# Start-up of a conditioned ternary feed-forward kernel: conditions loaded first, the second block's gathers moved, some work moved to ScalarE, a shorter alpha

## The chip, the core and the metric

The kernel runs on one core of one Trainium2 chip. The core has five engines that run side by side[...]: PE (TensorE, matrix products), DVE (VectorE), ACT (ScalarE), POOL (GpSimd) and SP (SyncE, which here only issues DMAs). [...] The metric is the time of one execution on the device in microseconds; the median over three runs was 1069.36 us, the lowest 1067.48 and the highest 1070.88.

## What is computed

A batch `x` of 128 x 64 x 512 floats is multiplied, sample by sample, with a 64 x 64 matrix that a condition index picks out of a table of 200. The result goes through a feed-forward network of width 512 - 2048 - 512 whose two weight matrices are first made ternary: each weight becomes -alpha, 0 or +alpha. The output of the network is rounded to 15 levels and added to `x`.

```python
def ternarize(W, threshold):
    absW = jnp.abs(W)
    delta = threshold * jnp.max(absW)
    mask = absW > delta
    n = jnp.maximum(jnp.sum(mask), 1)
    alpha = jnp.sum(jnp.where(mask, absW, 0.0)) / n
    Wt = alpha * jnp.sign(W) * mask
    return W + jax.lax.stop_gradient(Wt - W)

h = einsum('bct,bcd->bdt', x, weights[conditions])
h = gelu(ternary_linear(h, W1, b1), exact)
y = ternary_linear(h, W2, b2)
scale = max(abs(y)) / 7 + 1e-8
out = x + clip(round(y / scale), -7, 7) * scale
```

Alpha needs a maximum over the whole matrix (for delta), then a count and a sum over what lies above it. Since sum(|W| over the mask) = sum(relu(|W| - delta)) + n * delta, alpha can be written as sum(relu) / n + delta.

## The kernel before

**Blocks.** The 128 samples are 16 blocks (`NB`) of 8 samples; a block is 4 pairs (`PAIRS`) and 512 columns (`BLK`). For a block, `mix` multiplies each pair's `x` by a block-diagonal matrix `diag` that holds two condition matrices; `hi` and `lo` split the product into two parts of reduced precision (ACT copies, DVE subtracts). Layer 1 has 16 steps (`hc`, `NH` = 16) of 8 matmuls, one per 128 hidden units; ACT's `bend` applies the gelu with `alpha[1]` as scale and copies the result to its high part, and a subtraction on DVE or POOL (`low`) makes the low part. Layer 2 has 16 steps of 8 matmuls that add up in four banks of PSUM.

**Weights.** Both matrices are kept in small types and have to be widened to fp32r just before use: `widen1(n, hc)` for a step of layer 1 into one of four buffers `w1f`, `widen2(n, hc)` for one of layer 2 into one of four buffers `w2f`. All these widenings are POOL's before the change. A buffer comes free when the matmul four steps earlier has read it.

**Block 0 is a ramp.** No step can start until W1's threshold is known, so block 0 has an order of its own, written out by hand; every engine's instructions keep the order in which the program makes them (`InOrder`). SP loads W1 (four groups of 1 MB, `nat1`), the first `x`, then W2. PE runs 54 products on constants (`idle`) while DVE reduces W1 to its maximum and ACT makes signs and magnitudes. `fetch` is a gather of one pair's condition matrices, an indirect DMA that POOL issues from indices `rows`, which DVE works out of `conditions`; `place` copies a gathered pair into `diag` in two halves. Then, for W1: `mask1` (|W| > delta), `signed1` (mask times sign, the ternary matrix), `count1` (PE sums the mask), `above1` (ACT sums relu(|W| - delta)) and `alpha_1`. The products of layer 1 (`early`) do not need alpha, only the gelu after them does; five PSUM slots hold products that wait, so `early(k)` needs the gelu of step k - 5.

**After alpha** a loop over `hc` 5 to 15 (lines 639 to 645) issues `early(hc)`, the widening of step hc + 2, the bend of step hc - 4, and in `behind(hc)` the preparation of W2 on DVE: its maximum (`largest2`), delta, and `signed2(g)`, the ternary form of group g in two instructions over 128 x 2048. Even steps' `low` is POOL's in this ramp, odd steps' is DVE's. Layer 2 of block 0 follows as a loop of 14 steps (lines 658 to 683), in which DVE still makes groups 2 and 3 of W2, ACT keeps both matrices in fp8 (`kept`) and counts W2 (`count2`), and the next block's four pairs are mixed (`condition(1, j)`) at steps 5, 7, 9 and 11. Block 1 then starts with its layer 1.

**What the change touches.** The load of `conditions` (line 127, issued by ACT), the four calls `fetch(1, j)` (lines 558, 569, 576) with their `place` (line 624, steps 6 to 9 of the ramp's loop), W1's fourth sum, which DVE makes with a product of magnitude and mask (lines 593 to 602) while ACT makes the other three, `widen1` (line 383), `alpha_1` (lines 488 to 501), `sign1(3)` (line 580), `early(3)` (line 605), the two first `widen2` (lines 634 to 637).

Of the kernel before, what the change touches and what calls it, by code (L numbers as in the profile page):

```python
# [29 lines left out]
F32 = mybir.dt.float32  # L30
# [6 lines left out]
ALU = mybir.AluOpType  # L37
AX = mybir.AxisListType
PSUM = bass.MemoryType.PSUM

P = 128
# [17 lines left out]
def tile_cond_ternary_ffn(  # L59
# [12 lines left out]
    pe, act, dve, pool, sp = (  # L72
        InOrder(tc, e) for e in (nc.tensor, nc.scalar, nc.vector, nc.gpsimd, nc.sync)
    )
    B, C, T = x.shape
# [4 lines left out]
    PAIRS = 4  # L80
    BLK = PAIRS * P
    NB = B // (2 * PAIRS)
    NG = 4
# [6 lines left out]
    const = ctx.enter_context(tc.tile_pool(name="const", bufs=1))  # L90
# [3 lines left out]
    ps_c = ctx.enter_context(tc.tile_pool(name="ps_c", bufs=2, space=PSUM))  # L94
# [29 lines left out]
    first = big.tile([P, 4, P], F32, tag="big", name="first")  # L124
    cond_i, cond_f, wrap = (first[:, i, : B // 2] for i in range(3))
    cond_i = cond_i.bitcast(I32)
    act.dma_start(out=cond_i, in_=conditions)


    nat1, nat2 = [], []  # L130
# [4 lines left out]
    for g in range(NG):  # L135
        w = big.tile([P, GH, T], F32, tag="big", name=f"nat1_{g}")
# [6 lines left out]
    for g in range(NG):  # L143
        w = big.tile([P, GH, T], F32, tag="big", name=f"nat2_{g}")
# [40 lines left out]
    def fetch(n, j):  # L185

        pair = n * PAIRS + j
        wg = gather.tile([P, D], F32, tag="wg", name=f"wg_{pair}")
        pool.indirect_dma_start(
            out=wg[:, :],  # L190
            out_offset=None,
            in_=table,
            in_offset=bass.IndirectOffsetOnAxis(ap=rows[:, pair : pair + 1], axis=0),
        )
        return wg

    def place(j, wg):
        for h in range(2):
            pool.tensor_copy(diag[half_of(h), j, h * D : (h + 1) * D], wg[half_of(h), :])
# [49 lines left out]
    def alpha_of(w, sums, count):  # L249

        dve.tensor_scalar(count, count, 1.0, None, ALU.max)
        dve.reciprocal(count, count)
        alpha = const.tile([P, 1], F32, name=f"alpha_{w}")
        dve.tensor_tensor(alpha, sums, count, ALU.mult)
        return alpha

    def flat(w):
        return w.rearrange("p a b -> p (a b)")
# [3 lines left out]
    masks = [big.tile([P, 2, WCH], BF16, tag="big", name=f"masks_{i}") for i in range(2)]  # L262
    terns = [big.tile([P, 2, WCH], BF16, tag="big", name=f"terns_{i}") for i in range(2)]
    junk = big.tile([P, 2, WCH], BF16, tag="big", name="junk")
    above, above_last = junk[:, 0, :], junk[:, 1, :]
    top_1 = const.tile([P, sum(map(len, PIECES))], F32)
    sums1 = const.tile([P, NG], F32)

    def group1(tiles, g):
        return tiles[g // 2][:, g % 2, :]  # L270

    def sign1(g):
        act.activation(group1(signs, g), flat(nat1[g]), AF.Sign)
# [9 lines left out]
    mags = []  # L283
# [54 lines left out]
    def signed1(g, part=slice(0, WCH)):  # L338
        dve.tensor_tensor(
            group1(terns, g)[:, part],  # L340
            group1(masks, g)[:, part],
            group1(signs, g)[:, part],
            ALU.mult,
        )

    def count1(g, number, first, final):
        n = number.shape[1]
        for i in range(WCH // n):
            pe.matmul(
                out=number,  # L350
                lhsT=ones_b,
                rhs=group1(masks, g)[:, i * n : (i + 1) * n],
                start=(first and i == 0),
                stop=(final and i == WCH // n - 1),
            )
# [22 lines left out]
    def widen1(n, hc):  # L378

        if n == 0:  # L380
            w = w1f[hc % 4]
            g, i = divmod(hc, GH)
            pool.tensor_copy(flat(w), group1(terns, g)[:, i * T : (i + 1) * T])
        else:
            w = w1f[hc % 2]
            pool.tensor_copy(flat(w), w1t[:, hc])
        wide1[n, hc] = w

    def widen2(n, hc):
        if n == 0 and hc < NH - LAG:  # L390
            w = w2f[hc % 4]
        elif n == NB - 1 and hc == NH - 1:

            w = flat(w1f[0])
        else:
            w = w2f[hc % 2]
        if n == 0 and hc < NH - LAG:
            g, i = divmod(hc, GH)
            pool.tensor_copy(w, group1(terns2, g)[:, i * T : (i + 1) * T])
        else:  # L400
            pool.tensor_copy(w, w2t[:, hc])
        wide2[n, hc] = w
# [33 lines left out]
    def layer2(n, hc, js=range(PAIRS)):  # L436
        two = hidden[n, hc]
        w = wide2[n, hc]
        if n not in ypsum:
            ypsum[n] = [  # L440
                ps_y.tile([P, T], F32, tag=f"py{j}", name=f"py{j}_{n}") for j in range(PAIRS)
            ]
        for j in js:
            for k in range(2):
                pe.matmul(
                    out=ypsum[n][j],
                    lhsT=two[k][:, j * P : (j + 1) * P],
                    rhs=w,
                    start=(hc == 0 and k == 0),
                    stop=(hc == NH - 1 and k == 1),  # L450
                )
# [19 lines left out]
    def early(hc, between=None):  # L471

        slot = (hc + 1) % 5
        if slot < 2:
            ph = ps_h.tile([P, BLK], F32, tag="ph", name=f"ph_0_{hc}")
        else:
            ph = ps_y.tile([P, BLK], F32, tag=f"py{slot - 2}", name=f"ph_0_{hc}")
        layer1(0, hc, ph, 2 if hc == 0 else 1, between)
        waiting[hc] = ph
# [8 lines left out]
    def alpha_1():  # L488

        count = const.tile([P, 1], F32, name="count1")  # L490
        dve.tensor_reduce(count, number, AX.X, ALU.add)
        yield
        total = ps_c.tile([P, NG], F32, tag="pc", name="total1")
        pe.matmul(out=total, lhsT=ones_f, rhs=sums1, start=True, stop=True)
        count_last = const.tile([P, 1], F32, name="count1_last")
        dve.tensor_reduce(count_last, number_last, AX.X, ALU.add)
        kept = const.tile([P, 1], F32, name="kept1")
        dve.tensor_reduce(kept, total, AX.X, ALU.add)
        dve.scalar_tensor_tensor(kept, count, delta1, kept, ALU.mult, ALU.add)
        dve.tensor_tensor(count, count, count_last, ALU.add)  # L500
        alpha[1] = alpha_of("w1", kept, count)

    top_2 = const.tile([P, NG], F32)
    delta = []
# [50 lines left out]
        alpha[2] = alpha_of("w2", both[:, 0:1], both[:, 1:2])  # L555


    fetched = [fetch(1, 0)]
    mask1(0, parts1[0])
    signed1(0, parts1[0])  # L560
    widen1(0, 0)
# [4 lines left out]
    hi0(3)  # L566
    lo0(2)
    lo0(3)
    fetched += [fetch(1, 1)]
    early(0)  # L570
    early(1)
    mask1(0, parts1[1])
    signed1(0, parts1[1])
    widen1(0, 2)
    widen1(0, 3)
    fetched += [fetch(1, j) for j in range(2, PAIRS)]
    abs1(3)
    for g in range(NG - 1):
        above1(g)
    sign1(3)  # L580
    number = ps_y.tile([P, T // 2], F32, tag="py3", name="number")
    count1(0, number, True, False)
    mask1(1)
# [3 lines left out]
    mask1(3)  # L587
    early(2)
    count1(1, number, False, False)
    count1(2, number, False, True)  # L590
    number_last = ps_c.tile([P, T // 2], F32, tag="pc", name="number_last")
    count1(3, number_last, True, True)
    dve.tensor_tensor_reduce(
        out=above_last,
        in0=flat(mags[3]),
        in1=group1(masks, 3),
        scale=1.0,
        scalar=0.0,
        op0=ALU.mult,
        op1=ALU.add,  # L600
        accum_out=sums1[:, 3:4],
    )
    find = alpha_1()
    next(find)
    early(3, lambda: next(find, None))
    signed1(2)
    widen1(0, 5)
    early(4)
    early_bend(0)
# [10 lines left out]
    def behind(hc):  # L620
        if 5 <= hc < 5 + NG:
            largest2(hc - 5)
        if 6 <= hc < 6 + PAIRS:
            place(hc - 6, fetched[hc - 6])
        if hc == 9:
            signed1(3)
        if hc == 11:
            delta.extend(next(find))
            signed2(0)
        if hc == 12:  # L630
            low(0, 1)
            low(0, 3)
            signed2(1)
        if hc == 14:
            widen2(0, 0)
        if hc == 15:
            widen2(0, 1)

    for hc in range(5, NH):
        ahead(hc)  # L640
# [17 lines left out]
    for hc in range(NH - LAG):  # L658
        if hc + 2 < NH - LAG:
            widen2(0, hc + 2)  # L660
        layer2(0, hc)
        if hc == 0:
            signed2(2)
        if hc == 1:
            for i in (13, 14, 15):
                low(0, i)
        if hc < NG:
            kept(w1t, hc, terns)
        if hc == 3:
            signed2(3)  # L670
        if hc == 4:
            two_next = parts(1)
            w2t = big.tile([P, NH, T], F8, tag="big", name="w2t")
        if 4 <= hc < 4 + 2 * NG:
            g = (hc - 4) // 2
            if hc % 2 == 0:
                count2(g)
            else:
                kept(w2t, g, terns2)
        if hc in (5, 7, 9, 11):  # L680
            j = (hc - 5) // 2
            condition(1, j, pair_of(x_next, j), two_next)
            sum2(j)
    cond[1] = two_next
# [401 lines left out]
```

## Time and profile before

| What | Value |
|---|---|
| median of three runs | 1069.36 us |
| the profiled execution's own time | 1069.97 us |
| its span | 1067.9 us |
| PE busy | 991.2 us, 93% of the span |
| DVE busy | 613.4 us, 57% |
| ACT busy | 610.0 us, 57% |
| POOL busy | 635.3 us, 59% |
| first matmul of layer 1 in block 0 | 22.57 us after the span's start |
| alpha of W1 written | 35.86 us |
| first matmul of layer 2 in block 0 | 61.58 us |
| first matmul of block 1 | 92.33 us |

A row of a timeline gives the start in us from the span's start, the duration, the engine, line of the program, operation, tiles and shapes, how many instructions are merged into the row, and in brackets how long the engine had been idle and what ended that. Nearly all instructions pass through one helper on line 55, so the tile names tell them apart, not the line. `wf` stands for the widened weights of both layers, `py` for the sums of layer 2, `ph` for those of layer 1, `terns` for the ternary matrices, `wg` for a gathered pair of condition matrices, `h` for the split gelu outputs. [...]

### The profile page before, as it was taken

What the parts mean: (1) busy time and instruction counts of PE and PEld (TensorE: products, weight loads), DVE (VectorE), ACT (ScalarE), POOL (GpSimd) and SP (SyncE); (2) the same over time, 40 slices, a digit from 0 to 9 for tenths busy, and PEclk for the clock granted to TensorE, in tenths of its full rate; (3) what the DMA queues carried; (4) which work ended last, traced back from release to release, by engine and by line L of the source; (5) the groups of instructions that cost most, each with busy time, mean ns of one, the idle gap of its engine ahead of it and who ended that gap; (6) DMA issues with size and microseconds to landing.
All of it is one profiled execution on the core that took longest, in us unless ns stands there. A gap on an engine that the chain in (4) does not pass through costs nothing.

```text
span 1067.9 us, 16731 instructions
## 1 busy us (share of the span) xinstructions
PE 991.2 (93%) x5765; PEld 866.0 (81%) x5765; DVE 613.4 (57%) x1080; ACT 610.0 (57%) x1038; POOL 635.3 (59%) x1019
## 2 busy tenths in 40 slices
PE   8989999999999999999999999999999999999400
PEld 4778889999999999999999999999898888888300
DVE  6996736565656656565666655666655223231682
ACT  6875446656666666666666665666555334334481
POOL 4884747576666667576666767576664435333242
PEclk9999999999999999999999999999999999999855
DMA  9100010000000010101000010100001010041899
GB/s 369 46 21 1 14 32 5 30 15 22 23 23 23 14 32 5 31 15 30 16 22 24 14 32 4 34 13 30 16 21 42 3 40 6 1 148 31 301 412 367
DMA packets 26611, 62.20 MB, mean 58 GB/s; under 512 B 3488, under 2 KB 3488, under 8 KB 25760
## 3 DMA queue, kind: packets, MB, share of 16 engines
q1 hardware_dynamic: 19728, 42.22, 11.7%
q0 software_dynamic: 6656, 18.88, 4.6%
q8 instruction: 47, 0.77, 0.3%
q14 instruction: 36, 0.29, 0.1%
q10 hardware_dynamic: 144, 0.03, 0.0%
HBM read 44.34 MB, written 16.78 MB: 57 GB/s over the span
## 4 chain that ended last, share of the span: by engine, by line
PE 88%; DMA 3%; POOL 3%; DVE 2%; ACT 1%; issue 1%; SPq 1%; POOLq 0%; DVEq 0%; ACTq 0%
PE py L55 44%; PE xy L55 16%; PE z L55 12%; PE ph L55 11%; PE pc L55 5%; DMA xt<-in_x 2%; POOL wf L55 2%; DVE y L55 1%; ACT diag L55 1%; POOL wg L55 1%; POOL h L55 1%; SPq L55 1%; DMA wg<-in_L_cond_weights,rows 1%; DMA first<-in_itok_B 0%; POOL diag L55 0%
## 5 line engine op out<-in xcount | busy, mean ns | idle before, releaser
L55 PE MATMUL py<-wf,h 128*128 128x512 f32 x2048 | 532.6, 396 | 3.6 <-POOL wf L55 2.7
L55 PEld LDWEIGHTS py<-wf,h 128*128 128x128 f32 x2048 | 366.4, 189 | 68.8 <-POOL wf L55 3.2
L55 DVE TENSOR_TENSOR h<-ring,h 128x512 fp32r<-128x512 f32 x249 | 193.7, 780 | 184.0 <-ACT h L55 184.0
L55 POOL CAST wf<-w2t 128x512 fp32r<-128x512 fp8e4 x242 | 174.4, 721 | 151.7 <-PE py L55 147.7
L55 ACT ACTIVATE ring<-ring,b1t,alpha_w 128x512 f32<-128x512 f32 x176 | 144.4, 820 | 97.7 <-DVE ring L55 97.7
L55 POOL CAST wf<-w1s 128x256 fp32r<-128x256 fp8e4 (+1 forms) x264 | 133.8, 511 | 109.8 <-PE xy L55 80.6
L55 POOL CAST wf<-w1t 128x256 fp32r<-128x256 fp8e4 (+1 forms) x240 | 157.1, 659 | 56.3 <-PE ph L55 45.3
L55 ACT CAST h<-ring 128x512 fp32r<-128x512 f32 x256 | 158.9, 621 | 8.2
L55 PE MATMUL ph<-x,wf 128*128 128x512 f32 (+1 forms) x648 | 158.5, 389 | 1.1 <-POOL wf L55 1.0
L55 ACT ACTIVATE ring<-ph,b1t,alpha_w 128x512 f32<-128x512 f32 x80 | 62.3, 779 | 145.5 <-PE ph L55 141.9
L55 PEld LDWEIGHTS ph<-x,wf 128*128 128x128 f32 x648 | 119.7, 188 | 27.9 <-POOL wf L55 3.0
L55 DVE TENSOR_TENSOR ring<-xy,ring 128x256 f32<-128x256 f32 (+1 forms) x176 | 97.4, 553 | 64.2 <-PE xy L55 64.2
L55 PEld LDWEIGHTS xy<-xt,wf 128*128 128x128 f32 x704 | 107.6, 189 | 14.1
L55 PE MATMUL xy<-xb,wf 128*128 128x256 f32 x704 | 112.4, 282 | 0.0
L55 PE MATMUL xy<-xt,wf 128*128 128x256 f32 x704 | 111.8, 282 | 0.0
L55 PEld LDWEIGHTS xy<-xb,wf 128*128 128x128 f32 x704 | 102.3, 190 | 7.6
L55 ACT COPY ring<-xy 128x256 f32<-128x256 f32 x176 | 65.0, 369 | 68.1 <-PE xy L55 68.1
L55 PE MATMUL z<-xt,wf 128*128 128x256 f32 x704 | 98.6, 283 | 0.0
L55 ACT COPY ring<-z 128x512 f32<-128x512 f32 x88 | 51.7, 588 | 73.6 <-DVE h L55 73.0
L55 PEld LDWEIGHTS z<-xt,wf 128*128 128x128 f32 x704 | 90.5, 191 | 0.0
L55 DVE TENSOR_TENSOR xt<-x_quarters,xt 128x512 fp32r<-128x512 f32 x44 | 33.8, 768 | 91.0 <-ACT xt L55 91.0
L55 POOL DMA_INDIRECT wg<-in_L_cond_weights,rows x64 | 76.3, 1193 | 14.9 <-DVE rows L55 4.7
(106 smaller groups left out, 860.4 us busy)
## 6 DMA issues: line engine op xcount, KB each, us to landing
xt<-in_x SPq DMA_DIRECT2D x36, 512.0 KB, 9.0
out<-y POOLq DMA_DIRECT2D x30, 512.0 KB, 13.1
x_quarters<-in_x SPq DMA_DIRECT2D x48, 256.0 KB, 2.6
nat<-in_L_ffn_W SPq DMA_DIRECT2D x6, 1024.0 KB, 6.2
nat<-in_L_ffn_W SPq DMA_DIRECT2D x3, 512.0 KB
wg<-in_L_cond_weights,rows POOLq DMA_INDIRECT x64, 2.7
w1t<-in_x SPq DMA_DIRECT2D x4, 256.0 KB, 2.6
w2t<-in_x SPq DMA_DIRECT2D x4, 256.0 KB, 2.6
```

The lines of the kernel that those rows point to most:

```text
L55: return lambda *args, **kw: self._tc.keep_in_program_order(make(*args, **kw))
```

## The change

The load of `conditions` moves from ACT's queue to the head of SP's. The gathers of block 1 leave the ramp; they are issued in steps 0 to 3 of layer 2 of block 0 and placed in steps 4 to 7, and `condition(1, j)` and `sum2(j)` move one step back, to 6, 8, 10 and 12. W1's fourth sum is made by ACT like the other three, and `sign1(3)` moves behind it to step 6 of the ramp's loop. The widenings of steps 7, 9, 11, 13 and 15 of layer 1 in block 0 are ACT's. All four counts add into one bank, and alpha is sum * (1 / count) + delta, with the reciprocal taken before the sum is there. `early(3)` comes ahead of the last two counts, and `signed1(2)` ahead of the last steps of alpha. The first two `widen2` are issued one step earlier in the ramp's loop.

```diff
-    act.dma_start(out=cond_i, in_=conditions)
+    sp.dma_start(out=cond_i, in_=conditions)
...
-            pool.tensor_copy(flat(w), group1(terns, g)[:, i * T : (i + 1) * T])
+            src = group1(terns, g)[:, i * T : (i + 1) * T]
+            if hc > 6 and hc % 2 == 1:
+                act.copy(flat(w), src)
+            else:
+                pool.tensor_copy(flat(w), src)
...
         dve.tensor_reduce(count, number, AX.X, ALU.add)
+        dve.tensor_scalar(count, count, 1.0, None, ALU.max)
+        dve.reciprocal(count, count)
         yield
         total = ps_c.tile([P, NG], F32, tag="pc", name="total1")
         pe.matmul(out=total, lhsT=ones_f, rhs=sums1, start=True, stop=True)
-        count_last = const.tile([P, 1], F32, name="count1_last")
-        dve.tensor_reduce(count_last, number_last, AX.X, ALU.add)
         kept = const.tile([P, 1], F32, name="kept1")
         dve.tensor_reduce(kept, total, AX.X, ALU.add)
-        dve.scalar_tensor_tensor(kept, count, delta1, kept, ALU.mult, ALU.add)
-        dve.tensor_tensor(count, count, count_last, ALU.add)
-        alpha[1] = alpha_of("w1", kept, count)
+        alpha[1] = const.tile([P, 1], F32, name="alpha_w1")
+        dve.tensor_scalar(alpha[1], kept, count, delta1, ALU.mult, ALU.add)
...
-    fetched = [fetch(1, 0)]
...
-    fetched += [fetch(1, 1)]
...
-    fetched += [fetch(1, j) for j in range(2, PAIRS)]
     abs1(3)
-    for g in range(NG - 1):
+    for g in range(NG):
         above1(g)
-    sign1(3)
...
-    count1(2, number, False, True)
-    number_last = ps_c.tile([P, T // 2], F32, tag="pc", name="number_last")
-    count1(3, number_last, True, True)
-    dve.tensor_tensor_reduce(
...
-    )
+    early(3)
+    count1(2, number, False, False)
+    count1(3, number, False, True)
     find = alpha_1()
     next(find)
-    early(3, lambda: next(find, None))
     signed1(2)
+    next(find, None)
...
-        if 6 <= hc < 6 + PAIRS:
-            place(hc - 6, fetched[hc - 6])
+        if hc == 6:
+            sign1(3)
...
-        if hc == 14:
-            widen2(0, 0)
-        if hc == 15:
-            widen2(0, 1)
+        if hc in (13, 14):
+            widen2(0, hc - 13)
...
         layer2(0, hc)
+        if hc < PAIRS:
+            fetched.append(fetch(1, hc))
+        elif hc < 2 * PAIRS:
+            place(hc - PAIRS, fetched[hc])
...
-        if hc in (5, 7, 9, 11):
-            j = (hc - 5) // 2
+        if hc in (6, 8, 10, 12):
+            j = (hc - 6) // 2
```

## The prediction

> **What bounds the kernel now.** I read the page first (PE is 93% busy, and 88% of the chain that ended last), then the chain of waits in order of time, then the timeline of the first 95 us. From 92.33 us on, where block 1 starts, the chain is PE matmuls end to end, and the change touches nothing there. So the end moves by what the start of block 1 moves: everything has to be read from the ramp.
>
> ```profile
> PE 88%; DMA 3%; POOL 3%; DVE 2%; ACT 1%; issue 1%; SPq 1%; POOLq 0%; DVEq 0%; ACTq 0%
> ```
>
> In the ramp PE stands still where POOL's widened weights come late, most of all ahead of layer 2. The timeline there shows why they are late:
>
> ```profile
> 53.41 2.79 DVE L55 TENSOR_TENSOR h<-ring,h 128x512 fp32r<-128x512 f32 x2
> ...
> 53.93 1.73 POOL L55 TENSOR_TENSOR h<-ring,h 128x512 fp32r<-128x512 f32 x1
> ...
> 55.60 1.07 POOL L55 CAST wf<-terns 128x512 fp32r<-128x512 bf16 x1
> 56.12 1.63 DVE L55 TENSOR_SCALAR junk<-nat,minus_w 128x2048 bf16<-128x2048 f32 x1
> ...
> 56.64 2.27 POOL L55 TENSOR_TENSOR h<-ring,h 128x512 fp32r<-128x512 f32 x1
> ...
> 57.79 3.27 DVE L55 SCALAR_TENSOR_TENSOR terns<-nat,delta_w,junk 128x2048 bf16<-128x2048 f32 x1
> 58.85 3.69 POOL L55 CAST wf<-terns 128x512 fp32r<-128x512 bf16 x2
> ...
> 61.58 1.89 PE L55 MATMUL py<-wf,h 128*128 128x512 f32 x5 [2.74 <-POOL wf L55]
> ```
>
> DVE and POOL take turns. The cast ends at 56.67 and the DVE row that began at 56.12 ends 1.08 later (57.75); POOL's low part ends 1.16 after that (58.91), DVE's next 2.15 after that (61.06), the next cast 0.46 later, and PE starts. Each "long" instruction is mostly a wait for the other engine. The **exclusive prices** are thus 1.08 for `signed2`'s first instruction, 2.15 for its second, 0.54 for a low part on DVE (56.20 minus 55.66), 1.16 for one on POOL, 0.46 for a cast. While DVE is full, from 49.6 to 77 us, POOL gets one instruction per DVE instruction.
>
> The gap costs twice. The windows around it show the granted clock in the column behind the five engines:
>
> ```profile
> 58.60:61.60 3.00, 0.26 (x3) 0.03 (x1) 3.00 (x2) 2.69 (x3) 3.00 (x3) 1.00 0.00 0
> 61.60:65.80 4.20, 4.20 (x12) 3.29 (x13) 4.20 (x5) 4.20 (x4) 4.20 (x4) 0.59 0.41 125
> 65.80:68.00 2.20, 2.20 (x11) 1.83 (x10) 2.16 (x2) 1.71 (x1) 2.20 (x3) 1.00 0.00 0
> ```
>
> After 2.74 us without work PE ran 4.2 us at 0.59: 4.2 x 0.41 = **1.7 us lost**.
>
> **The change, part by part.**
>
> *Conditions on SP.* The DMA took 5.3 us to land from ACT's queue, beside W1's; at the head of an idle SP queue it should take no more than the 2.6 of a 256 KB quarter of `x`. SP's whole queue (W1, x, b1, W2, b2) is issued 0.4 later, one issue. The indices come 2.5 to 3 us earlier, so gathers and `place` are done before they are needed. DVE's maximum no longer waits for the indices (it began at 7.21, with W1 there at 5.9): 0.9 earlier. But PE's 54 constant products still end at 16.95, where the transposition of the maximum started before too, so delta stays. What gains is the mixing: it waited for `diag` at 18.16 and 19.53, and can now run 17.2 to 20.9. Layer 1 then begins at 20.9 instead of 22.57; its second half waits for the fourth low part, 22.3 instead of 23.82. **Gain 1.5 us** at that point. If the conditions land no earlier, this goes.
>
> *Alpha.* PE is full from there: step 1, four counts of 0.85 and steps 2 and 3 end at 32.6. ACT's four sums (2.1 each) end at 31.9, hidden behind that. Then DVE's count (0.42), two small ones (0.4), `signed1(2)` (1.2, newly ahead of alpha), two small ones (0.4): alpha at 35.2, against 35.86. The product of magnitude and mask (2.29) and three tiny instructions are gone, but 1.2 is put in their place and PE's step 3 in front: **gain 0.7**.
>
> *ACT in the loop.* Before, gelu and copy took 1.33 per step against PE's 1.82, with room. New are five casts (no such row on ACT; nearest are `h<-ring` at 0.62, stepping by 0.54, and a four times larger `w1t<-terns` at 1.9; I take 0.55) and `sign1(3)` (1.9) inside the loop. `early(8)` waits for gelu 3, behind that sign: 0.9 of PE idle. `early(11)` lands at 48.7, against 48.60: **the gain is spent**. Copy 8 ends at 35.2 + 9 x 1.34 + 1.9 + 4 x 0.55 = 51.4, against 49.36. The five casts leave POOL (five times 0.6 to 2.7), so the ramp's last steps no longer stall for POOL (0.58 and 2.74 before): `early(15)` ends at 57.8, and layer 2 begins at 58.5, when gelu 13 has freed its bank. **Gain 3.1**, and without the long gap also the 1.7 of slow clock.
>
> *Gathers into layer 2.* Here it is given back. Delta of W2 comes with `early(11)`, so DVE's full stretch starts at about 50.2, no earlier than before (49.59). Then, in turns: first `signed2` 1.1 + 2.25, low 8 1.15, 0.54, cast 0.46, 0.54, low 10 1.15, 1.1, cast 0.46, 2.15, low 12 1.15, 0.54, cast 0.46: the third `widen2` is there at 63.3, and step 2 of layer 2, wanted at 62.1, starts then. Now the four gathers stand between the next four casts. Their rows before:
>
> ```profile
> 28.80 2.24 POOL L55 DMA_INDIRECT wg<-in_L_cond_weights,rows  x1
> 31.35 2.72 POOL L55 DMA_INDIRECT wg<-in_L_cond_weights,rows  x1 [0.30 <-issue]
> ...
> 108.40 2.70 DVE L55 TENSOR_TENSOR w1s<-w1t 128x2048 fp8e4<-128x2048 fp8e4 x1
> 109.10 2.83 POOL L55 DMA_INDIRECT wg<-in_L_cond_weights,rows  x1
> 111.94 0.99 POOL L55 CAST wf<-w1t 128x512 fp32r<-128x512 fp8e4 x1
> ```
>
> Undisturbed a gather takes 0.97; at 109.10 it waits until DVE ends (111.10) and needs 0.83 more, in which DVE's next instruction starts, and the cast behind it waits for that one. So each gather costs a turn. From 63.3: gathers end at 64.7, 67.6, 70.8, 73.6, and the casts between them at 65.6, 69.4, 71.7, 75.5. Layer 2's steps 3 to 6 start at those four times instead of every 1.82: PE idles 0.5, 2.0, 0.5, 2.0. Step 6 starts at 75.5. From there eight steps (14.56) and four mixings (3.56) run without a stall (places cost two times 0.3, DVE is idle by then). The last mixing is now followed by one step of layer 2 (1.82) instead of two, which has to cover its high and low part (0.59 and 0.69 plus two hand-overs, some 1.45): it just does, and if ACT or DVE is late by more than 0.35, block 1 waits for the rest. Block 1 at **93.7, against 92.33: 1.4 later**.
>
> [...] The row at 109.10, a two-input DVE instruction, has the gather wait; I follow the row.
>
> **The sum:** 1069.97 for the profiled execution plus 1.4 is 1071.4. That execution lies 0.6 above the median, so on the median's scale I forecast **1070.8**: no change that can be told, since 0.3% (3.2 us) is what a measurement of this kernel tells from none.
>
> **Rivals.**
>
> *Faster: the feed keeps up.* If gathers fit between DVE's instructions, layer 2 runs through from 63.4: 12 x 1.82 + 3.56 gives 88.8, 3.5 earlier: 1065.8. If casts 1 and 2 come early too, from 57.8 straight through it is 86.9: 1064. For it: layer 2 is ready 3.1 earlier and the slow clock is gone. Against it: the row at 109.10, and eight more POOL instructions where it already takes turns.
>
> *Slower: the clock drops again.* Same starvation, but the two gaps of 2.0 count as idle. Each would cost 1.7 if PE were the limit behind it; the first is half hidden by the next wait for a cast, the second, ahead of step 6, is not. 1070.8 + 1.7 is 1072.5, with both nearly 1073.5. It decides if a gap of 2.0 suffices. [...] here 2.74 was enough, [...] and 2.0 is not safe.
>
> *The head gains nothing:* conditions land after 5 us all the same, or W1's later issue shows. Then alpha is about 1 later and all behind it: 1071.8 to 1072.3.
>
> **Numbers.** My forecast's own range is 1069 to 1072.5 (the turns are known to a few tenths each, the ACT cast to 0.1, five times). Chances: forecast 0.43 with the head case in it, feed keeps up (wholly or partly) 0.36, slow clock 0.21. The range for 8 in 10 reaches to both: 1065 to 1073.5. Of the faster case about five sixths passes 3.2 us; of the slower one most stays near the bound. Faster 0.30, same 0.50, slower 0.20.
>
> **What would show it.** Right: conditions landed by 3.5, mixing from about 17, alpha near 35, no PE gap of more than 1 us between 49 and 58, layer 2 from about 58, and gaps for `wf` of 1 to 2 us at its steps 2 to 6, with gathers of 1.4 to 2 us before them. Wrong: gathers of 1.0 there and casts every 1.8 (faster), or a granted clock under 1 between 65 and 80 (slower). Block 1's first matmul, 92.33 before, carries the verdict: whatever it moves, the end moves.

## The result, and the profile after

| What | Before | After |
|---|---|---|
| median of 20 runs each | 1069.30 us (1067.18 to 1070.92) | 1070.05 us (1069.09 to 1071.02) |
| ratio after to before | | 1.0010, 95% interval 1.0004 to 1.0017 |
| profiled execution, own time / span | 1069.97 / 1067.9 us | 1070.15 / 1068.3 us |
| first matmul of layer 1 in block 0 | 22.57 us | 20.70 us |
| alpha of W1 written | 35.86 us | 34.87 us |
| first matmul of layer 2 in block 0 | 61.58 us | 57.50 us |
| first matmul of block 1 | 92.33 us | 93.12 us |

The change costs 0.75 us of 1069. That is 0.1%, just clear of none by the interval of this comparison and far under the 0.3% that the forecast took as its bound; by that bound it is no change, as forecast. Inside the ramp much moved. Layer 2 of block 0 starts 4.1 us earlier, and then takes 35.62 us to reach block 1 instead of 30.75, or instead of some 29.05 if the 1.7 us of half clock are taken out of before. So 5.8 us were won ahead of layer 2 or with the clock, and 6.6 given back inside it. Behind block 1's first matmul all profiles of this document take 974.9 to 976.4 us to the end of the span, so the start of block 1 carries the result to within some 1.5 us.

The chain that ended last, from the page of after. It is still PE, now 91% where it was 88%; POOL's share fell from 3% to 1%.

```profile
PE 91%; DMA 3%; DVE 2%; ACT 2%; POOL 1%; issue 1%; SPq 1%; POOLq 0%; DVEq 0%; ACTq 0%
```

PE's timeline of after: start, duration, operation, how many matmuls (8 are one step), and in brackets the idle time and what ended it.

```profile
20.70 1.32 PE L55 MATMUL ph<-x,wf 128*128 128x256 f32 x9
22.34 2.94 PE L55 MATMUL ph<-x,wf 128*128 128x256 f32 x15 [0.33 <-DVE x L55]
...
35.88 2.08 PE L55 MATMUL ph<-x,wf 128*128 128x512 f32 x8 [1.28 <-ACT ring L55]
...
42.71 5.73 PE L55 MATMUL ph<-x,wf 128*128 128x512 f32 x24 [0.37 <-ACT ring L55]
48.30 9.36 PE L55 MATMUL ph<-x,wf 128*128 128x512 f32 x40
57.50 3.79 PE L55 MATMUL py<-wf,h 128*128 128x512 f32 x16
62.91 4.15 PE L55 MATMUL py<-wf,h 128*128 128x512 f32 x16 [1.62 <-POOL wf L55]
67.44 2.12 PE L55 MATMUL py<-wf,h 128*128 128x512 f32 x8 [0.38 <-POOL wf L55]
71.06 4.13 PE L55 MATMUL py<-wf,h 128*128 128x512 f32 x16 [1.50 <-POOL wf L55]
76.66 1.16 PE L55 MATMUL pc<-diag,xt 128*128 128x128 f32 x8 [1.47 <-POOL diag L55]
...
93.12 1.98 PE L55 MATMUL ph<-x,wf 128*128 128x512 f32 x8
```

Up to 57 us the longest stop is now 1.28 us, behind alpha; the stop of 2.74 us ahead of layer 2 is gone. In its place stand four stops inside layer 2, three for `wf` (a widened weight) and one for `diag` (a placed condition). POOL's timeline in that stretch shows the cause of all but the first:

```profile
63.01 1.25 POOL L55 DMA_INDIRECT wg<-in_L_cond_weights,rows  x1 [0.15 <-issue]
64.28 0.62 POOL L55 CAST wf<-terns 128x512 fp32r<-128x512 bf16 x1
65.06 1.71 POOL L55 DMA_INDIRECT wg<-in_L_cond_weights,rows  x1 [0.17 <-PE py L55]
66.77 0.62 POOL L55 CAST wf<-terns 128x512 fp32r<-128x512 bf16 x1
67.56 2.83 POOL L55 DMA_INDIRECT wg<-in_L_cond_weights,rows  x1 [0.17 <-issue]
70.39 0.62 POOL L55 CAST wf<-terns 128x512 fp32r<-128x512 bf16 x1
71.18 1.23 POOL L55 DMA_INDIRECT wg<-in_L_cond_weights,rows  x1 [0.17 <-issue]
72.41 0.62 POOL L55 CAST wf<-terns 128x512 fp32r<-128x512 bf16 x1
72.98 3.63 POOL L55 COPY diag<-wg 64x64 f32<-64x64 f32 x2
```

And DVE's timeline beside it:

```profile
66.68 2.86 DVE L55 SCALAR_TENSOR_TENSOR terns<-nat,delta_w,junk 128x2048 bf16<-128x2048 f32 x1
69.47 2.70 DVE L55 TENSOR_TENSOR h<-ring,h 128x512 fp32r<-128x512 f32 x3
72.09 2.03 DVE L55 TENSOR_SCALAR junk<-nat,minus_w 128x2048 bf16<-128x2048 f32 x1
74.16 2.35 DVE L55 SCALAR_TENSOR_TENSOR terns<-nat,delta_w,junk 128x2048 bf16<-128x2048 f32 x1
```

Read the third gather with it. It is issued at 67.56 and waits until DVE's row of 66.68 has ended (69.54), then works for 0.85 and ends at 70.39. Only then can the cast for step 5 (counted from 0) run, and PE starts step 5 at 71.06. The last row of POOL is the same wait for a `place`: its second half stands behind the DVE row of 74.16, ends at 76.61, and the mixing starts at 76.66.

### The profile page after: what moved, and what is told of

Its sections match the earlier page's. It is cut to its first block, busy times and chain, and to the rows that moved or that the text cites. A ratio compares the mean times of both kernels' runs of the same rounds, so it can differ in the third digit from the quotient of the medians.

```text
span 1068.3 us, 16722 instructions
## 1 busy us (share of the span) xinstructions
PE 990.0 (93%) x5764; PEld 864.0 (81%) x5765; DVE 610.8 (57%) x1075; ACT 614.4 (58%) x1045; POOL 629.5 (59%) x1014
## 4 chain that ended last, share of the span: by engine, by line
PE 91%; DMA 3%; DVE 2%; ACT 2%; POOL 1%; issue 1%; SPq 1%; POOLq 0%; DVEq 0%; ACTq 0%
PE py L55 43%; PE xy L55 16%; PE ph L55 13%; PE z L55 12%; PE pc L55 5%; DMA xt<-in_x 3%; PE idle L55 1%; DVE y L55 1%; ACT diag L55 1%; SPq L55 1%; POOL wg L55 0%; POOL diag L55 0%; ACT ring L55 0%; PE number L55 0%; DVE ymax L55 0%
```

## The experiments

My theory before the runs: two separate parts of the change gain (conditions, casts on ACT), and the gathers give it back, because each takes one of POOL's turns where POOL feeds PE. The rivals: the start-up parts gain nothing in truth, or what the gathers lose was lost anyway, to DVE's full stretch.

**The change without its move of the gathers.** Gathers, places and mixing stand where they stood before; all else is the change.

```diff
+    fetched = [fetch(1, 0)]
     mask1(0, parts1[0])
...
+    fetched += [fetch(1, 1)]
     early(0)
...
+    fetched += [fetch(1, j) for j in range(2, PAIRS)]
     abs1(3)
...
+        if 6 <= hc < 6 + PAIRS:
+            place(hc - 6, fetched[hc - 6])
...
-        if hc < PAIRS:
-            fetched.append(fetch(1, hc))
-        elif hc < 2 * PAIRS:
-            place(hc - PAIRS, fetched[hc])
...
-        if hc in (6, 8, 10, 12):
-            j = (hc - 6) // 2
+        if hc in (5, 7, 9, 11):
+            j = (hc - 5) // 2
```

> The changed kernel with the gathers, their placing and the mixing of block 1 back where they were before. Theory A (the gathers in layer 2 starve PE of widened weights, about 5 us of gaps between 57 and 78 us): those gaps go; PE alone would then reach block 1 at 88.3 us (62.9 plus 12 x 1.82 plus 3.56), but ACT's last high part comes only about 90, because its second count of W2 waits for DVE's last instruction on the shared junk tile; so block 1 at 89.5 to 91 instead of 93.1, the time 2 to 3.5 us under the changed kernel, about 1067. Theory B (the lost time is ACT's, which has more work in the ramp, and the gathers only fill waits): block 1 within 0.5 us of 93.1, about 1070.

Measured: 1066.84 us, ratio to before 0.9976 (0.9966 to 0.9986), 3.2 below the change. PE's timeline:

```profile
57.23 3.79 PE L55 MATMUL py<-wf,h 128*128 128x512 f32 x16
62.67 7.55 PE L55 MATMUL py<-wf,h 128*128 128x512 f32 x32 [1.65 <-POOL wf L55]
...
89.03 0.47 PE L55 MATMUL ph<-x,wf 128*128 128x512 f32 x1 [0.68 <-ACT x L55]
```

Layer 2 begins where it does in the change (57.23 to 57.50), and so does its third step. Behind that the stops are gone: 31.80 us from the start of layer 2 to block 1 instead of 35.62. The move of the gathers, with their placing and the mixing that follows it, is what gives the gain back. A new limit shows at the end: block 1 waits 0.68 for ACT. ACT's timeline says why:

```profile
69.40 1.91 ACT L55 ACTIVATE junk<-terns 128x2048 bf16<-128x2048 bf16 x1 [1.66 <-DVE terns L55]
...
76.26 1.91 ACT L55 ACTIVATE junk<-terns 128x2048 bf16<-128x2048 bf16 x1 [2.58 <-DVE terns L55]
...
88.30 0.59 ACT L55 CAST x<-pc 128x512 fp32r<-128x512 f32 x1
```

The rows that wait are `count2`, which write into `junk`, DVE's scratch for `signed2`. ACT stands for 1.66 and 2.58 us, and the copy that block 1 needs ends only at 88.89.

**The same, with another scratch for the counts.**

```diff
-            junk[:, g % 2, :], group2(g), AF.Square, accum_out=sums2[:, 1, g : g + 1]
+            group1(signs, g), group2(g), AF.Square, accum_out=sums2[:, 1, g : g + 1]
```

> As undo_gathers, and ACT's counts of W2 write their unused output over the signs of W1 instead of the junk tile that DVE uses. Theory A with ACT as the next limit: ACT no longer waits for DVE, PE is the limit, block 1 at 88 to 89 us, about 1065.3, 1 to 2 us under undo_gathers. If ACT's wait is no limit: the same as undo_gathers within 0.5 us.

Measured: 1065.57 us, 0.9964 (0.9952 to 0.9976); block 1 at 87.96, with no wait for ACT; the two waits of ACT for DVE are gone from the trace. The tile shared as scratch was worth 1.3 us once the gathers were away.

**Only the move of the gathers**, put into the kernel before.

> The kernel before with nothing but the gathers, placing and mixing moved as in the change. Theory A: the ramp gains about 0.7 us at alpha (no gathers between the casts), layer 2 loses 3 to 5 us between steps 2 and 7, partly hidden behind the half clock that was there anyway: 1 to 3 us slower than before, about 1071. Theory B: no slower than before, 1068.5 to 1069.5.

Measured: 1070.62 us, 1.0015 (1.0008 to 1.0021); block 1 at 92.79. Layer 2 begins at 56.84, 4.7 earlier than before, since POOL has lost four gathers and eight copies from the ramp; then it stops for 1.88 at step 2, 0.81 at step 5 and 1.45 ahead of the first mixing, and runs 3.41 us at half clock. So the move by itself also gains ahead of layer 2 and loses more in it.

**Only the conditions on SP**, put into the kernel before.

> The kernel before with nothing but the conditions on SP's queue. If the head's gain is passed on: mixing from 17.2 instead of 18.2, alpha 1.0 to 1.5 us earlier, and layer 2 earlier by the same since POOL and DVE follow: about 1068. If what sets the start of layer 2 does not hang on the head (a full POOL or DVE): alpha earlier, block 1 within 0.5 us of 92.3, 1069.3.

Measured: 1066.84 us, 0.998 (0.997 to 0.999). Alpha at 34.04, layer 2 at 59.78, block 1 at 91.83. The stop of 2.74 us ahead of layer 2 is still there. The profiled execution took 1069.24, the longest of its 14 runs (the shortest 1065.19), and PE worked 6.1 us at half clock in it: 3.1 us lost.

**Only the five casts on ACT**, put into the kernel before.

> The kernel before with nothing but the five widenings moved to ACT. If POOL's queue is what delays layer 2 of block 0: two casts fewer ahead of its first step (1.6 and 1.1 us before), so it starts 2 to 3 us earlier[...]; then DVE's chain for W2 takes over at step 2 or 4: 1 to 3 us faster than before, 1066.5 to 1068. If DVE and ACT set that start anyway: within 0.5 us of before.

Measured: 1067.71 us, 0.9981 (0.9973 to 0.9989). Layer 2 begins at 59.09, its gap at step 2 is 0.75 us, and block 1 (90.59) waits 1.25 us for ACT's copy of `x`. Its trace runs 3.4 us at half clock in the first mixing, so alpha comes at 37.13 there, 1.3 later than before, and layer 2 is earlier in spite of that. The wait for ACT comes with the casts; the alpha part alone (below) has none there.

**Only the alpha part**, put into the kernel before: the fourth sum on ACT, one bank for the counts, the short formula, the new places of `early(3)`, `signed1(2)` and `sign1(3)`.

> The kernel before with nothing but the alpha part: ACT's fourth sum, one bank for the counts, the shorter formula, step 3 ahead of the last two counts, the fourth sign inside the loop. By the sum of the prediction PE's step 3 (1.9 us) ahead of the counts and the ternary product ahead of alpha undo what the formula saves: alpha between 35.5 and 36.5 instead of 35.9, and the sign in the loop costs up to 0.9: 1069 to 1070.5. If the shorter formula is what helps: alpha 1 to 2 us earlier, 1067 to 1068.

Measured: 1070.53 us, 1.0012 (1.0005 to 1.0020): no gain, rather 1.1 us of loss. Alpha is written at 35.98 (35.86 before). The product of magnitude and mask is gone from DVE, but the counts now end behind step 3 on PE, at 33.6, and `signed1(2)` (1.2 us) runs ahead of the last steps of alpha; the next step of PE then stops for 1.28 us.

**The change with conditions back on ACT's queue.**

```diff
-    sp.dma_start(out=cond_i, in_=conditions)
+    act.dma_start(out=cond_i, in_=conditions)
```

> The changed kernel with the conditions back on ACT's queue. If all behind the head hangs on it: alpha and block 1 about 1 us later, 1071. If the turns of DVE and POOL in layer 2 absorb it: within 0.4 us of the changed kernel, 1070.

Measured: 1071.89 us, 1.003 (1.0018 to 1.0042), so by the medians the load is worth 1.8 us inside the change and 2.4 alone. In its trace layer 1 and all that follows, every stop of layer 2 too, lies some 1.1 later (block 1 at 94.24): what the head wins goes through undiminished as long as the same engines bind behind it. The two profiled executions differ by only 0.9 us; why the medians differ by more was not settled.

**Gathers in the one place where POOL is idle.** Without them POOL has nothing to do from 28.9 to 35.3 us; the four gathers go there, and the places stay where the change put them.

```diff
     widen1(0, 5)
+    fetched += [fetch(1, j) for j in range(PAIRS)]
     early(4)
...
-        if hc < PAIRS:
-            fetched.append(fetch(1, hc))
-        elif hc < 2 * PAIRS:
+        if PAIRS <= hc < 2 * PAIRS:
             place(hc - PAIRS, fetched[hc])
```

> The changed kernel with the four gathers issued by POOL right after the widening of step 5, in the 6.5 us in which it waits for the first gelu; their placing stays in steps 4 to 7 of layer 2. If the gathers alone take the turns: no gaps at steps 3 to 6 of layer 2, block 1 at 89 to 89.5 (ACT's last high part, as in undo_gathers), 1066 to 1066.5. If the placing costs as much as the gathers: the gap of 1.5 us ahead of the first mixing stays, block 1 at 90.5 to 91.5, 1067.5 to 1068.5.

Measured: 1066.55 us, 0.9977 (0.9969 to 0.9985); block 1 at 88.68. POOL's timeline:

```profile
29.00 0.98 POOL L55 DMA_INDIRECT wg<-in_L_cond_weights,rows  x1 [0.15 <-issue]
30.29 0.94 POOL L55 DMA_INDIRECT wg<-in_L_cond_weights,rows  x1 [0.31 <-issue]
31.54 0.95 POOL L55 DMA_INDIRECT wg<-in_L_cond_weights,rows  x1 [0.30 <-issue]
32.79 1.37 POOL L55 DMA_INDIRECT wg<-in_L_cond_weights,rows  x1 [0.30 <-issue]
```

The same four instructions that took 1.23 to 2.83 us in layer 2 take 0.94 to 1.37 here, and PE waits for none of them. From layer 2's start to block 1 it is 32.36 us instead of 35.62: 3.3 of the 6.6 are the gathers alone. (Of the 4.4 us by which block 1 comes earlier in this trace the other 1.2 were there before any gather was issued; the section on the hardware says from what.) With the places still late, one wait of 0.98 for a cast is left at step 8, beside the stop at step 2.

**Taking the stop at step 2 away.** On the kernel with the other scratch: the low part of step 12, which POOL makes ahead of the third `widen2`, is issued at step 5 of layer 2.

```diff
+        late = hc == NH - 4
+        bend(0, hc, waiting.pop(hc), two, hf, pool if on_pool and not late else None)
+        if late:
+            open_low[0, hc] = lambda: pool.tensor_tensor(two[1], hf, two[0], ALU.subtract)
...
+        if hc == 5:
+            low(0, NH - 4)
```

> undo_gathers_scratch, with the low part of step 12 issued by POOL in step 5 of layer 2, no longer between the second and third widening of W2. If taking turns with DVE is what makes the third widening late (gap of 1.8 us at step 2): it comes one pair of turns, 1.2 to 2 us, earlier, the gap shrinks under 0.5: 1064. If DVE's ternary W2 is what it waits for: 1065.5 as in undo_gathers_scratch.

Measured: 1064.42 us, 0.9947 (0.9932 to 0.9961); six steps of layer 2 run from 57.77 without a stop, and block 1 begins at 87.11. The stop of 1.62 at step 2 is a matter of POOL's order, not of the gathers.

**All together.** The last kernel with the two steps of alpha ahead of `signed1(2)` again, and 50 constant products instead of 54.

```diff
-    for _ in range(54):
+    for _ in range(50):
...
-    signed1(2)
     next(find, None)
+    signed1(2)
```

> low12_late, with the third ternary product of W1 behind alpha again and 50 instead of 54 constant products. If each is on the path: delta 0.9 us earlier, alpha 1.2 us earlier on top, the gap of 1.4 us after step 4 closes; part of it returns at the sign in the loop: 1062 to 1063.5. If ACT's full queue from alpha on is the limit, only the time at which alpha comes counts, and the end still moves by the 2 us. If neither reaches block 1: 1064.

Measured: 1062.93 us (1062.32 to 1063.32), 0.9932 (0.9919 to 0.9945): the shortest of all, 6.5 below before and 7.1 below the change. PE's timeline:

```profile
33.79 2.09 PE L55 MATMUL ph<-x,wf 128*128 128x512 f32 x8 [0.15 <-ACT ring L55]
...
55.40 3.82 PE L55 MATMUL py<-wf,h 128*128 128x512 f32 x16
59.71 7.55 PE L55 MATMUL py<-wf,h 128*128 128x512 f32 x32 [0.49 <-POOL wf L55]
...
85.22 1.98 PE L55 MATMUL ph<-x,wf 128*128 128x512 f32 x8
```

The stop of 1.28 behind alpha is 0.15, and alpha is written at 32.78. Block 1 begins 7.9 us earlier than in the change. The two edits were not run apart. By the traces alpha comes 16.49 us after the last constant product instead of 17.62, so the order is worth 1.1 us there, and four products fewer are an estimated 0.9 (0.215 us each); 0.5 of the 2.0 returns as the stop at step 2, and the medians differ by 1.5.

**The clock.** The kernel before, with eight products on constants that nobody reads put on PE behind the last step of layer 1, where it stood for 2.74 us.

```diff
+    filler = ps_h.tile([P, T], F32, tag="ph", name="filler")
+    for _ in range(8):
+        pe.matmul(out=filler, lhsT=ones_b, rhs=group1(masks, 0)[:, :T], start=True, stop=True)
     w1t = big.tile([P, NH, T], F8, tag="big", name="w1t")
```

> The kernel before with eight products on constants (1.7 us) behind layer 1's last step in block 0, in the 2.7 us in which PE waits for the first widening of W2; nothing reads them. If the half clock after that gap is on the path: no stretch at half clock, layer 2's first six steps in 10.9 us instead of 12.6, 1.0 to 1.7 us faster than before, about 1068, and runs closer together than those of before. If POOL's and DVE's turns set the pace there anyway: within 0.4 us of before.

Measured: 1067.41 us (1066.79 to 1068.40), 0.9991 (0.9983 to 0.9999), beside a before of 1067.96 measured with it. By the times alone this is weak: in the other comparisons before lay 1.3 to 1.5 us higher. The trace is plain: the granted clock is 1.00 from 58.90 to 65.70, and the first six steps of layer 2 take 11.1 us (61.09 to 72.22) where before they take 12.6 (61.58 to 74.20). The windows of the two, with the busy time of PE, its weight loads, DVE, ACT and POOL, and behind these the granted clock; first of before, then with the added products:

```profile
58.90:62.30 3.40, 0.72 (x3) 0.64 (x4) 3.40 (x3) 3.37 (x4) 3.40 (x3) 1.00 0.00 0
62.30:65.73 3.43, 3.43 (x10) 2.67 (x9) 3.43 (x4) 3.43 (x3) 3.43 (x4) 0.50 0.50 153
```

```profile
58.90:62.30 3.40, 2.40 (x11) 1.37 (x10) 3.40 (x3) 3.37 (x4) 3.40 (x3) 1.00 0.00 0
62.30:65.70 3.40, 3.40 (x16) 2.64 (x16) 3.40 (x4) 3.40 (x3) 3.40 (x3) 1.00 0.54 154
```

## Why the prediction was right

Forecast 1070.8, measured 1070.05, and block 1 at 93.12 for 93.7. The mechanism it named carries the result: undoing the gathers' move alone gives 3.2 us back, and putting the gathers where POOL is idle gives 3.5. But two of its terms were wrong, by 1.7 and 2.0 us, with opposite signs, and layer 2 began 1.0 us earlier than forecast. That these errors nearly cancel, so that the number came out within 0.8 us, is luck.

- **Conditions.** Right. They land 1.7 us after their issue (at most 2.6 was taken), the mixing runs from 17.21 (17.2), layer 1 from 20.70 (20.9), and its second half waits at 22.3. As forecast delta did not move: the maximum is ready at 16.07, but its transposition stands behind the constant products until 17.10. The rival that the head gains nothing falls.
- **Alpha.** 34.87 for 35.2. The gain is not the formula's: alone the alpha part is worth nothing (+1.1 us). What makes alpha earlier in the change is the earlier head: with the conditions back on ACT's queue alpha is at 36.00, and with the conditions alone on SP's it is at 34.04, 0.8 earlier than in the change. That `signed1(2)` and step 3 take the place of what goes was seen; that they eat all of it and more was not.
- **ACT in the loop.** The casts take a step of 0.52 for 0.55. The stop behind the sign is 0.37 for 0.9, and copy 8 ends at 50.93 for 51.4. Layer 2 begins at 57.50, not 58.5, just as gelu 13 ends (57.46), as the forecast had it.
- **Gathers into layer 2.** This is the term whose parts were mis-sized. Counted from start to start against 1.82 per step, PE lost 1.77 ahead of step 2, 0.89 by step 4 and 1.80 by step 5: 4.5, where 1.16 + 0.5 + 2.0 + 0.5 + 2.0 = 6.2 was forecast. The sentence that failed is "the cast behind it waits for that one". In layer 2 the cast behind each gather took its bare 0.62; the DVE instruction that starts beside the end of a gather is short there (a low part of 0.68) or itself waits for the cast (2.03 for the `TENSOR_SCALAR` of 72.09, 1.28 for that of 65.37), and the second gather ended only 0.12 after the DVE row of 65.37.
- **Places.** "Places cost two times 0.3, DVE is idle by then" failed the other way: the last `signed2` ran until 76.51, the second half of a `place` waited for it, and PE lost 1.96 (5.60 less two steps) ahead of the first mixing. So 6.4 in all for 6.2, by other parts.
- **Last mixing.** One step of layer 2 behind it covered its high and low part: block 1 follows without a stop.
- **Slower clock.** The rival did not happen: no half clock in the change between 58 and 95 us (1.00 granted throughout). It could have: the same gathers alone had it (last section), so this too is in part luck.
- **The row at 109.10.** Rightly followed: the gather beside the two-input row of 66.68 waited too, 1.98 of its 2.83. The trace does not tell what in the gather waited.

The parts alone sum to -2.4 (conditions), -1.8 (casts), +1.1 (alpha) and +1.4 (gathers), -1.7 together, while the whole is +0.75. They are not additive. Casts alone bring the start of layer 2 forward by 2.5 us and the gathers' move alone by 4.7, since each takes away the stop of 2.74 ahead of it; the whole change brings it forward by 4.1, so what is won there is won once. ACT as the next limit at block 1, seen in two of the variants, may add to this; how much belongs to each was not told apart. The fifth part, the first two `widen2` one step earlier, was neither tried alone nor undone, and the casts and the alpha part were not undone in the change.

## What to carry to other kernels

An instruction that is moved off a busy stretch has to be moved into an idle one: look for the idle rows of its own engine, and where the trace shows its instructions waiting for those of a busy neighbour, add that wait to the bare duration (up to 1.98 us for a gather of 0.97 here). Undo each part of a change by itself as well as trying it alone, since two parts can remove the same wait and win it only once. A scratch tile that two engines wrote was a wait between them (ACT stood for 1.66 and 2.58 us), though nobody reads it.

## What the runs showed of the hardware

**Half clock came behind windows in which PE was little busy.** Ahead of the last 70 us the granted clock was 0.50 in before for 3.41 us (62.31 to 65.73), with only the conditions moved for 6.80 (59.10 to 65.90), with only the gathers moved for 3.41, and with only the casts moved for 3.40. In the 3.40 us ahead of it PE worked for 0.72 in before (above) and for 1.35 with only the conditions moved (55.70 to 59.10). Only the gathers moved, and only the casts moved:

```profile
59.28:62.69 3.41, 1.53 (x8) 0.95 (x7) 3.41 (x3) 3.41 (x3) 3.25 (x3) 1.00 0.00 0
62.69:66.10 3.41, 3.41 (x9) 2.67 (x10) 3.41 (x4) 3.21 (x2) 3.24 (x3) 0.50 0.43 163
```

```profile
15.90:19.30 3.40, 1.31 (x9) 0.94 (x9) 2.59 (x8) 2.95 (x2) 1.53 (x3) 1.00 1.03 413
19.30:22.70 3.40, 3.40 (x19) 3.40 (x18) 1.15 (x2) 1.17 (x2) 2.88 (x8) 0.50 1.01 422
```

The change itself stays at 1.00 behind 2.07 (59.22 to 62.63) and behind 1.91 (69.45 to 72.86), before with the added products behind 2.40 (above), and the change with the conditions back on ACT's queue behind 1.77:

```profile
61.21:64.62 3.41, 1.77 (x8) 1.16 (x7) 3.41 (x4) 3.38 (x4) 3.26 (x3) 1.00 0.05 3
64.62:68.03 3.41, 3.41 (x15) 2.36 (x13) 3.37 (x4) 3.41 (x3) 3.23 (x4) 1.00 0.52 160
```

Of these eight windows, those with 1.53 us of PE or less were followed by half clock, and those with 1.77 or more were not. The length of the longest stop does not part them: with only the casts moved it was 1.51, with half clock behind it, and in the change 1.62 (ahead of step 2), with none. A stretch costs an estimated 1.7 us where PE is busy all through it (3.41 at 0.50). Behind a window at half clock it was different: with only the conditions moved, one with 2.7 us of PE (6.12 in both windows, less 3.40) was followed by a second at 0.50. What else counts was not shown.

**The constant products end at different times, and the ramp feels it.** In before's profile they start every 0.43 us up to 7.62 and every 0.22 from 7.88; in the change's the pace doubles at 8.03. These are the constant products of two kernels that are alike up to there, the one with the gathers where POOL is idle and the one with the low part of step 12 moved (53 and 54 because a record can be missing):

```profile
2.97 13.11 PE L55 MATMUL idle<-junk,ones_b 128*128 128x512 bf16 x53 [2.97 <-POOL junk L55]
```

```profile
2.96 14.61 PE L55 MATMUL idle<-junk,ones_b 128*128 128x512 bf16 x54 [2.96 <-POOL junk L55]
```

They end at 16.08 and 17.57. In the change and in its four variants with the conditions on SP's queue and the same order at alpha, alpha is written 17.61 to 17.64 us after that end, and layer 2 begins 22.6 after alpha: there the ramp up to layer 2 hangs on the end of the constant products, and a comparison of two traces carries up to 1.5 us that no edit made. The medians, and stretches between two events of one trace, tell more here than single starts do. The kernel before spreads over 5.3 us (1066.7 to 1072.0 in all its runs), and kernels without the stop of 2.74 ahead of layer 2 over 0.6 to 2.6, in fewer runs each; each profile shows one execution, so where the spread comes from was not shown.

**A gather beside a busy DVE.** In the change, the gather of 67.56 ended 0.85 after the two-input DVE row of 66.68, for which it had stood 1.98, and that of 71.18 ended 0.84 after a low part that ended at 71.57, for which it had stood 0.39. The one at 65.06 ended 0.12 after the `TENSOR_SCALAR` of 65.37, which has one tensor input and began after it. But not every such row held a gather up. In before, DVE and POOL:

```profile
23.13 0.69 DVE L55 TENSOR_TENSOR x<-pc,x 128x512 fp32r<-128x512 f32 x1 [0.20 <-ACT x L55]
```

```profile
23.23 0.97 POOL L55 DMA_INDIRECT wg<-in_L_cond_weights,rows  x1
```

Three more of before took 0.95 to 0.98 beside DVE's reductions of W1 (7.21 to 16.25), and with the gathers where POOL is idle three took 0.94 to 0.98 and one 1.37. What parts these cases was not shown.
